# Tokens in a used block sum, row blocks normalised in place, and a fourth buffer of raw weights, in a gated cross-attention and FFN kernel

## The chip, the cores and the metric

The kernel runs on one core of a Trainium2 chip. The metric is the device time of one execution in microseconds (us), median of several runs. PE is the matrix engine (TensorE), DVE the vector engine, ACT the scalar engine, POOL GpSimd and SP the engine that here only issues transfers. [...]

## The reference

There are 8 batches of 256 tokens of width 1024, each with 256 feature rows. A cross-attention with a gated residual is followed by a feed-forward layer with fake-quantised (rounded to 8-bit steps) inputs and weights. Cut to what matters:

```python
# attention, per batch
Q = layernorm(x) @ Wq.T + bq
K = ctx @ Wk.T + bk
attn = softmax(Q @ K.T / sqrt(1024))
x = x + tanh(g_xattn) * (attn @ ctx)
# feed-forward; fake_quant rounds each row to multiples of max|row| / 127
xq = fake_quant(layernorm(x))
h = silu(xq @ fake_quant(w_gate).T) * (xq @ fake_quant(w_up).T)
x = x + tanh(g_ffn) * (fake_quant(h) @ fake_quant(w_down).T)
```

The inner width of the feed-forward layer is 2752, in 22 blocks of up to 128.

## The kernel before

The kernel multiplies the two projection matrices once: M = Wq^T Wk (the tile `mt`), so that scores are x M ctx^T plus bias terms. M is made from seven half-size products of blocks A (of Wq) and B (of Wk) and their sums, in the order P1, a second product, P6, P5, P4, P3, P7 (lines 361 to 481). The sum S1 = A21 + A22 is an input of P5 (line 383) and is not read after it. `usum` and `v_bc` hold bias-weighted column sums; `usum` is read by `bias_columns` in the first two steps of P3.

Up to line 911 every instruction goes out in the order in which the program writes it (`manual_schedule`), on every engine and every queue. This order is by hand, and so is the place of each piece of background work in it.

The background work is the quantisation of the feed-forward weights. `pieces` (lines 180 to 185) lists 92 of them: for every block of 128 rows a gate and an up piece, and, in between, for each of eight blocks of `w_down` three pieces of kind "max" and three of kind "store". `prepare()` (line 247) advances a software pipeline by one step. In step i, piece i-3 is stored (ACT takes the rounding constant off into `rq`, then either SP transposes `rq` into the resident weights, or ACT sends it to `wdq_dram`), piece i is loaded by SP into a `raw` buffer, and piece i-2 is scaled (DVE takes the absolute maximum of each row and the scale from it, POOL multiplies and rounds). For kind "max" only the maximum is taken; for kind "store" only POOL works, with the scale known. Three `raw` buffers are there, so the load of piece i waits until ACT has read piece i-3. The padding of the last `w_down` columns is a memset on POOL.

Before the batch loop, the first batch's tokens `x0` are loaded (line 441) into a tile of the pool `f_right` that has the tag "fn"; the first batch's features (line 600) use the same tag and so the same memory. Then the tokens are normalised and transposed into `xT` (PE transposes into a "tr" bank, of which there are two; ACT or DVE copies it out). The eight query products (`queries_product(j)`, line 499, eight accumulating groups of matmuls from `mt` and `xT`, each evacuated by ACT into H) follow at lines 604 to 617. Between them stand the prepare steps, the statistics of the next batch's tokens (DVE, with a root on ACT), their normalisation, and the transposes of the features into `fT`.

The batch loop (lines 643 to 693) overlaps batch b's softmax and attention with batch b+1's query products. `softmax_stage` (line 619) runs the scores of the two row blocks on PE. Between them PE transposes the next tokens and ACT copies them to `xT`; DVE takes the row maximum (`shift`) and ACT the exponentials (`numerators`). ACT works in order: the first exponential stands between the copies of the first and the second token block. `tokens_bias` (line 426) multiplies tokens by `v_bc` and sums; its product is thrown away, and only the sum is kept. `residual` adds the attention output to the tokens `xr`; the result goes to `x2_dram` from POOL's queue. `steps` (line 575) normalises a row block of `xr` into a tile `y`, takes its scale and scales it; `store_steps` (line 590) has ACT turn it into `xq` (bf16) and sends it out. The second row block's `store_steps` is put off to the next batch (`waiting`). `y` has one buffer, which `scratch` (the thrown-away product) shares.

After the loop the last batch's softmax and attention are mixed with the first blocks of the feed-forward layer (lines 872 to 911). The feed-forward layer then runs to the end: gate and up products, their hidden values, and down products, for eight batches.

Of the kernel before, what the change touches and what calls it, by code (L numbers as in the profile page):

```python
# [9 lines left out]
F32 = mybir.dt.float32  # L10
# [17 lines left out]
def gated_xattn_ffn_kernel(  # L28
# [137 lines left out]
    if True:  # L166
        wraw = keep_scope.enter_context(tc.tile_pool(name="wraw", bufs=3, side=right))
        wkeep = keep_scope.enter_context(tc.tile_pool(name="wkeep", bufs=1, side=right))
# [56 lines left out]
        def prepare_store(i):  # L225
            src, kind, part, r = pieces[i]
            raw = raws.pop(i)
            if kind == "max":
                return
            rq = wraw.tile([P, D], BF16, name="rq", tag="rq", bufs=2)  # L230
            if src is w_down:
                cols = down_cols[part]
                w = cols.stop - cols.start
                nc.scalar.activation(rq[:, :w], raw[:, :w], AF.Identity, bias=nmagic)
                if part == len(down_cols) - 1:

                    nc.gpsimd.memset(rq[:, w : w + NFC * P - FF], 0.0)
                    w += NFC * P - FF
                nc.scalar.dma_start(
                    out=wdq_dram[r][:, cols.start : cols.start + w], in_=rq[:, :w]  # L240
                )
            else:
                n = rows_of(r)
                nc.scalar.activation(rq[:n], raw[:n], AF.Identity, bias=nmagic[:n])  # L244
                nc.sync.dma_start_transpose(out=chunk_of(kind, r), in_=rq[:n])

        def prepare(n=1):
            for _ in range(n):
                i = step[0]
                if 0 <= i - 3 < len(pieces):  # L250
                    prepare_store(i - 3)
                if i < len(pieces):
                    prepare_load(i)
                if 0 <= i - 2 < len(pieces):
                    prepare_scale(i - 2)
                step[0] += 1
# [8 lines left out]

        KH = KC // 2
        wqk_scope = ExitStack()
        wqk = wqk_scope.enter_context(tc.tile_pool(name="wqk", bufs=1))
# [47 lines left out]

        usum = wqk.tile([P, D], F32, name="usum")
        halves = [slice(h * HB, (h + 1) * HB) for h in range(NH)]
# [62 lines left out]
        for k in range(KH):  # L381
# [3 lines left out]
            add(C22[k], p5, C12[k])  # L385
            prepare()
        for k in range(KH):
            p4 = bank("a")
# [37 lines left out]
        def tokens_bias(b, tokens, prod):  # L426
# [8 lines left out]
        cq = {}  # L435
        f_right = keep_scope.enter_context(
            tc.tile_pool(name="f_right", bufs=1, side=right, reuse_waits="tile")
        )

        x0 = f_right.tile([P, NTT, D], F32, name="x0", tag="fn", bufs=1)  # L440
        nc.sync.dma_start(out=x0, in_=x[0].rearrange("(t p) d -> p t d", p=P))
        x0 = [x0[:, t, :] for t in range(NTT)]
        xT = f_right.tile([P, KC, NTT * P], F32, name="xT", tag="xT")
        stats = Rows()
# [130 lines left out]
        def steps(i, xr, stats):  # L575
            y = work.tile([P, D], F32, name="y", tag="y", bufs=1)
            normalise(y, xr, stats, i % NTT)
            scaled(i, y, nc.vector)
            return y

        def normalised_by_scalar(xr, stats, t):
            y = work.tile([P, D], F32, name="y", tag="y", bufs=1)
            nmr = small.tile([P, 1], F32, name="nmr", tag="nmr")
            nc.vector.tensor_scalar(
                nmr, stats.mv[:, t, 0:1], stats.rstd[:, t : t + 1], -1.0, ALU.mult, ALU.mult
            )
            nc.scalar.activation(y, xr, AF.Identity, bias=nmr, scale=stats.rstd[:, t : t + 1])
            return y

# [6 lines left out]
        def scratch():  # L596
            return work.tile([P, D], F32, name="prod", tag="y", bufs=1)


        load_features(0, f_right)  # L600
        xn = load_tokens(1, "xn")
        load_features(1, f_left)
        stats = Rows()
        for j in range(KC):
# [8 lines left out]
            if j in (4, 5):  # L613
                normalise(xn[j - 4], xn[j - 4], stats, j - 4)
            if j in (3, 4):
                features_transposed(0, 2 * j - 6, nc.scalar.copy)
                features_transposed(0, 2 * j - 5, nc.vector.tensor_copy)

# [18 lines left out]
        def queries_between(j):  # L637
            queries_product(j)
            if 0 < j < KC - 1:
                prepare()  # L640

        waiting = None
        for b in range(B - 1):
            nums = softmax_stage(b, xn)
            if waiting:
                store_steps(*waiting)
            prepare()
            queries_between(0)
            xr = load_tokens(b, "xr")
            tokens_bias(b + 1, xn, scratch)  # L650
            pT = numerators_transposed(nums[0][0])
            queries_between(1)
            pas = attend(b, pT)
# [218 lines left out]
    first = {"xq": load_quantised(0), "sx": sx01[:, 0:1, :], "h": []}  # L872
    xr = load_tokens(B - 1, "xr")
    nums = softmax_stage(B - 1, None)
    store_steps(*waiting)
    for r in range(KC):
        nc.sync.dma_start_transpose(
# [148 lines left out]
```

## Time and profile before

| what | value |
|---|---|
| median of 3 runs | 968.78 us (968.43 to 970.61) |
| the profiled execution, whole | 967.01 us |
| its span, first to last instruction | 964.8 us |
| mean granted PE clock | 0.996 of full speed |
| PE idle before 108 us / 108 to 144 / 144 to 476 / 476 to 530 / after 530 | 1.4 / 4.5 / 5.7 / 3.2 / 13.1 us |
| mean share of the 16 DMA engines from 108 to 144 / 144 to 476 us | 0.85 / 0.77 |
| load of a `raw` block, issue to landing | 4.6 us median, 8.3 at most |

The profile is of one execution, whose time is beside its span above; sums over the span are held against that execution. Rows of a timeline give the start and the duration of an instruction in us, its engine, its line, its operation, the tile written and the tiles read, and in brackets how long the engine stood idle before it and what released it. A row of the waits gives the engine and line that waited, what it waited for, the total in us, how many times, and the longest. The projection part ends at about 108 us, the query products ahead of the loop at about 144, the batch loop at about 476.

### The profile page before, as it was taken

The page shows a single profiled execution, that of the slowest core. Times are in us where ns is not written, and L with a number is a line of the kernel's source. Part 1 is how long each engine was busy: PE and PEld are TensorE (multiplying, and loading weights), DVE is VectorE, ACT ScalarE, POOL GpSimd, SP SyncE. Part 2 cuts the span into 40 slices and gives each one's busy share as a digit, 9 for nine tenths or more (in the row PEclk, how much of TensorE's full clock was granted, in tenths as well). Part 3 has the DMA queues.
Part 4 walks back from the last instruction along what each step waited for, and adds up shares of the span by engine and source line. Part 5 has one row for each costly group of instructions (what it writes and reads, how often), then busy time and mean ns, then how long its engine had stood idle before and what let it go on. Part 6 is the DMA issues. An engine that isn't in the chain of part 4 may idle for free.

```text
span 964.8 us, 14230 instructions
## 1 busy us (share of the span) xinstructions
PE 936.9 (97%) x5479; PEld 693.2 (72%) x5496; DVE 645.1 (67%) x1328; ACT 368.4 (38%) x650; POOL 153.5 (16%) x161
## 2 busy tenths in 40 slices
PE   9999989989999999999998899999999999999998
PEld 5444767868787878787877676858768586786854
DVE  5977645768586968777367756666576755767673
ACT  0122325444544535453537753423424143241420
POOL 0031211121221221223000002003030020302005
PEclk9999999999999999999999999999999999999999
DMA  9165976959596977858681611012120121201104
GB/s 347 68 144 181 264 178 190 295 188 314 173 299 203 291 238 249 272 194 256 174 164 34 120 23 65 24 22 89 22 86 3 22 88 23 88 1 45 44 1 153
DMA packets 125699, 135.93 MB, mean 141 GB/s; under 512 B 90241, under 2 KB 91521, under 8 KB 125633
## 3 DMA queue, kind: packets, MB, share of 16 engines
q1 hardware_dynamic: 112352, 104.36, 39.5%
q0 software_dynamic: 4784, 16.52, 4.5%
q10 hardware_dynamic: 8496, 14.16, 4.0%
q8 instruction: 43, 0.70, 0.3%
q14 instruction: 24, 0.19, 0.1%
HBM read 87.04 MB, written 26.74 MB: 118 GB/s over the span
## 4 chain that ended last, share of the span: by engine, by line
PE 78%; DVE 10%; DMA 6%; ACT 3%; issue 2%; SPq 1%; POOL 1%; ACTq 0%; DVEq 0%; POOLq 0%
PE ps_g L746 14%; PE ps_tr L746 14%; PE ps_g L503 11%; PE ps_s L839 6%; PE ps_a L839 6%; PE ps_s L503 6%; PE ps_a L550 6%; PE ps_s L521 4%; PE ps_s L308 3%; PE ps_a L308 3%; PE ps_tr L401 2%; DMA A<-in_L_xattn_Wq_dram 2%; DMA raw<-in_L_ffn_w_up_dram 1%; DMA xr<-x_dram 1%; DVE st L132 1%
## 5 line engine op out<-in xcount | busy, mean ns | idle before, releaser
L503 PE MATMUL ps_g<-xT,mt 128*128 128x256 f32 x640 | 146.4, 382 | 3.4 <-ACT xT L424 3.4
L757 ACT ACTIVATE g<-g,swg 128x256 f32<-128x256 f32 (+1 forms) x176 | 79.7, 499 | 159.3 <-DVE g L755 159.3
L503 PEld LDWEIGHTS ps_g<-xT,mt 128*128 128x128 f32 x640 | 121.0, 192 | 24.3 <-ACT xT L424 5.5
L839 PEld LDWEIGHTS <-hq 128*128 128x128 bf16 x726 | 71.4, 98 | 76.1
L859 POOL TENSOR_TENSOR o<-o,xr 128x512 f32<-128x512 f32 x31 | 39.9, 1288 | 395.3 <-DVE o L856 386.2
L767 DVE SCALAR_TENSOR_TENSOR h<-ps_tr,swu,g 128x256 f32<-128x256 f32 x160 | 70.3, 482 | 43.8 <-ACT g L757 40.6
L746 PE MATMUL ps_tr<-xqb,wuT_lo 128*128 128x256 bf16 x704 | 86.2, 276 | 3.4 <-DVE h L767 3.4
L209 POOL TENSOR_SCALAR raw<-raw,inv 128x1024 f32<-128x1024 f32 (+1 forms) x44 | 56.6, 1286 | 203.9 <-DVE inv L114 139.7
L503 PE MATMUL ps_s<-xT,mt 128*128 128x256 f32 x384 | 86.9, 379 | 0.0
L746 PE MATMUL ps_g<-xqb,wgT_lo 128*128 128x256 bf16 x704 | 84.7, 273 | 0.1
L781 DVE TENSOR_TENSOR acc<-acc,g 128x512 f32<-128x512 f32 (+2 forms) x88 | 56.6, 644 | 41.8 <-ACT g L771 41.0
L746 PE MATMUL ps_tr<-xqb,wuT_hi 128*128 128x256 bf16 x640 | 77.7, 273 | 1.3 <-DVE h L767 1.1
L746 PEld LDWEIGHTS <-wuT_lo 128*128 128x128 bf16 x704 | 69.6, 99 | 12.5 <-issue 3.7
L746 PE MATMUL ps_g<-xqb,wgT_hi 128*128 128x256 bf16 x640 | 77.7, 273 | 0.4 <-DVE g L755 0.4
L503 PEld LDWEIGHTS ps_s<-xT,mt 128*128 128x128 f32 x384 | 71.3, 190 | 8.8
L746 PEld LDWEIGHTS <-wgT_lo 128*128 128x128 bf16 x704 | 69.0, 98 | 9.9 <-issue 0.6
L244 ACT ACTIVATE rq<-raw,nmagic 128x1024 bf16<-128x1024 f32 (+1 forms) x44 | 50.5, 1148 | 65.4 <-POOL raw L209 58.7
L824 DVE TENSOR_TENSOR h<-h,bc 128x512 f32<-128x512 f32 x80 | 51.7, 687 | 28.0 <-ACT bc L819 28.0
L746 PEld LDWEIGHTS <-wuT_hi 128*128 128x128 bf16 x640 | 62.6, 98 | 9.1 <-issue 1.8
L746 PEld LDWEIGHTS <-wgT_hi 128*128 128x128 bf16 x640 | 62.6, 98 | 8.0 <-issue 0.7
L118 DVE TENSOR_REDUCE wam<-raw 128x1 f32<-128x1024 f32 (+1 forms) x44 | 53.1, 1208 | 19.0 <-DMA raw<-in_L_ffn_w_up_dram 18.7
L521 PE MATMUL ps_s<-fT,H 128*128 128x256 f32 x256 | 59.3, 380 | 1.3 <-ACT H L507 1.3
(179 smaller groups left out, 1337.8 us busy)
## 6 DMA issues: line engine op xcount, KB each, us to landing
raw<-in_L_ffn_w_down_dram SPq DMA_DIRECT2D x32, 512.0 KB, 5.3
raw<-in_L_ffn_w_gate_dram SPq DMA_DIRECT2D x21, 512.0 KB, 4.5
raw<-in_L_ffn_w_up_dram SPq DMA_DIRECT2D x21, 512.0 KB, 4.5
fn<-in_ctx_dram SPq DMA_DIRECT2D x8, 1024.0 KB, 8.2
xr<-in_x_dram SPq DMA_DIRECT2D x16, 512.0 KB, 5.5
x_dram<-xr POOLq DMA_DIRECT2D x16, 512.0 KB, 5.7
xr<-x_dram SPq DMA_DIRECT2D x32, 256.0 KB, 3.5
out_dram<-o POOLq DMA_DIRECT2D x31, 256.0 KB, 3.7
```

The source lines that it names most:

```text
L118: nc.vector.tensor_reduce(dst, src, AX.X, ALU.max, apply_absolute_value=True)
L209: nc.gpsimd.tensor_scalar(raw[:n], raw[:n], inv, MAGIC, ALU.mult, ALU.add)
L308: nc.tensor.matmul(pm, lhsT=a[:, c, k * P : (k + 1) * P], rhs=b[:, c, :], start=start, stop=stop)
L503: nc.tensor.matmul(ph, lhsT=mt[:, k, j * P : (j + 1) * P], rhs=xT[:, k, :], start=(k == 0), stop=(k == KC - 1),)
L521: nc.tensor.matmul(ps[:, :L], lhsT=H[:, j, t * P : (t + 1) * P], rhs=fT[:, j, :], start=(j == 0), stop=(j == KC - 1),)
L550: nc.tensor.matmul(pas[h], lhsT=pT[:, l, :], rhs=f_tiles[b][:, l, halves[h]], start=(l == 0), stop=(l == NLT - 1),)
L746: nc.tensor.matmul(pb[:, i, :], lhsT=w[:, k, :], rhs=block["xq"][:, k, :], start=(k == 0), stop=(k == KC - 1),)
L757: nc.scalar.activation(g[:n, i, :], g[:n, i, :], AF.Silu, scale=swg[:n, c : c + 1])
L767: nc.vector.scalar_tensor_tensor(h[:n, i, :], src, swu[:n, c : c + 1], g[:n, i, :], ALU.mult, ALU.mult)
L781: nc.vector.tensor_tensor(acc[:n, i, :], acc[:n, i, :], g[:n, i, :], ALU.max)
L824: nc.vector.tensor_tensor(h, h, ib.to_broadcast((P, 2, TB)), ALU.mult)
L839: nc.tensor.matmul(pds[t, half][:, cols], lhsT=hq[p][:, i, t * P : (t + 1) * P], rhs=wd[:, half * HB + cols.start : half * HB + cols.stop] ...
```

## The change

The first batch's tokens are loaded into the memory of S1, after P5 in program order, in two transfers. The first batch's features are loaded where the tokens were, and the second batch's in step j = 3 of the query products. The features' transposes are spread over j = 2 to 5, all copied by ACT. `f_right` and `xT` are made earlier, and `usum` becomes a view of `xT`.

`raw` gets a fourth buffer, and in a prepare step the load is issued ahead of the store. The padding is written by ACT as ones times zero.

`y` is gone: the normalisation and scaling of `xr` are done in place, and the thrown-away product of `tokens_bias` goes to the `xq` tile, in bf16. `tokens_bias` moves ahead of the put-off `store_steps`. The prepare step that came after `store_steps` moves behind the transpose of the numerators. The one behind query product 1 in the loop is dropped, and one is added behind query product 7. In the last batch the tokens are loaded after `store_steps` and not before the softmax stage.

```diff
--- before.py
+++ after.py
@@ -164,7 +164,7 @@
     order.enter_context(tc.manual_schedule())
     keep_scope = ExitStack()
     if True:
-        wraw = keep_scope.enter_context(tc.tile_pool(name="wraw", bufs=3, side=right))
+        wraw = keep_scope.enter_context(tc.tile_pool(name="wraw", bufs=4, side=right))
         wkeep = keep_scope.enter_context(tc.tile_pool(name="wkeep", bufs=1, side=right))
         mt = wkeep.tile([P, KC, D], F32, name="mt")
         u_col = wkeep.tile([P, KC], F32, name="u_col")
@@ -234,8 +234,9 @@
                 nc.scalar.activation(rq[:, :w], raw[:, :w], AF.Identity, bias=nmagic)
                 if part == len(down_cols) - 1:
 
-                    nc.gpsimd.memset(rq[:, w : w + NFC * P - FF], 0.0)
-                    w += NFC * P - FF
+                    pad = NFC * P - FF
+                    nc.scalar.activation(rq[:, w : w + pad], ones[:, :pad], AF.Identity, scale=0.0)
+                    w += pad
                 nc.scalar.dma_start(
                     out=wdq_dram[r][:, cols.start : cols.start + w], in_=rq[:, :w]
                 )
@@ -247,10 +248,10 @@
         def prepare(n=1):
             for _ in range(n):
                 i = step[0]
+                if i < len(pieces):
+                    prepare_load(i)
                 if 0 <= i - 3 < len(pieces):
                     prepare_store(i - 3)
-                if i < len(pieces):
-                    prepare_load(i)
                 if 0 <= i - 2 < len(pieces):
                     prepare_scale(i - 2)
                 step[0] += 1
@@ -264,6 +265,10 @@
 
 
         KH = KC // 2
+        f_right = keep_scope.enter_context(
+            tc.tile_pool(name="f_right", bufs=1, side=right, reuse_waits="tile")
+        )
+        xT = f_right.tile([P, KC, NTT * P], F32, name="xT", tag="xT")
         wqk_scope = ExitStack()
         wqk = wqk_scope.enter_context(tc.tile_pool(name="wqk", bufs=1))
 
@@ -314,7 +319,7 @@
 
 
 
-        usum = wqk.tile([P, D], F32, name="usum")
+        usum = xT[:, : D // (NTT * P), :].rearrange("p c t -> p (c t)")
         halves = [slice(h * HB, (h + 1) * HB) for h in range(NH)]
 
         def bias_sums(a, b, cs, c, half):
@@ -384,6 +389,13 @@
             combined(T4, T2, B21, ALU.subtract, k)
             add(C22[k], p5, C12[k])
             prepare()
+
+        x0 = [S1[:, 2 * t : 2 * t + 2, :] for t in range(NTT)]
+        for t in range(NTT):
+            nc.sync.dma_start(
+                out=x0[t], in_=x[0, t * P : (t + 1) * P, :].rearrange("p (c d) -> p c d", c=2)
+            )
+        x0 = [v.rearrange("p c d -> p (c d)") for v in x0]
         for k in range(KH):
             p4 = bank("a")
             product_of(p4, A22, k, T4)
@@ -433,14 +445,7 @@
             nc.vector.tensor_scalar(cq[b], cq[b], bqbk, None, ALU.add)
 
         cq = {}
-        f_right = keep_scope.enter_context(
-            tc.tile_pool(name="f_right", bufs=1, side=right, reuse_waits="tile")
-        )
-
-        x0 = f_right.tile([P, NTT, D], F32, name="x0", tag="fn", bufs=1)
-        nc.sync.dma_start(out=x0, in_=x[0].rearrange("(t p) d -> p t d", p=P))
-        x0 = [x0[:, t, :] for t in range(NTT)]
-        xT = f_right.tile([P, KC, NTT * P], F32, name="xT", tag="xT")
+        load_features(0, f_right)
         stats = Rows()
         for k in range(KH):
             p3 = bank("s")
@@ -573,19 +578,17 @@
                 nc.scalar.activation(y, y, AF.Identity, bias=magic, scale=inv)
 
         def steps(i, xr, stats):
-            y = work.tile([P, D], F32, name="y", tag="y", bufs=1)
-            normalise(y, xr, stats, i % NTT)
-            scaled(i, y, nc.vector)
-            return y
+            normalise(xr, xr, stats, i % NTT)
+            scaled(i, xr, nc.vector)
+            return xr
 
         def normalised_by_scalar(xr, stats, t):
-            y = work.tile([P, D], F32, name="y", tag="y", bufs=1)
             nmr = small.tile([P, 1], F32, name="nmr", tag="nmr")
             nc.vector.tensor_scalar(
                 nmr, stats.mv[:, t, 0:1], stats.rstd[:, t : t + 1], -1.0, ALU.mult, ALU.mult
             )
-            nc.scalar.activation(y, xr, AF.Identity, bias=nmr, scale=stats.rstd[:, t : t + 1])
-            return y
+            nc.scalar.activation(xr, xr, AF.Identity, bias=nmr, scale=stats.rstd[:, t : t + 1])
+            return xr
 
         def store_steps(i, y):
             b, t = divmod(i, NTT)
@@ -594,12 +597,10 @@
             nc.scalar.dma_start(out=xq_dram[b][t * P : (t + 1) * P, :], in_=xq)
 
         def scratch():
-            return work.tile([P, D], F32, name="prod", tag="y", bufs=1)
-
-
-        load_features(0, f_right)
+            return work.tile([P, D], BF16, name="prod", tag="xq", bufs=1)
+
+
         xn = load_tokens(1, "xn")
-        load_features(1, f_left)
         stats = Rows()
         for j in range(KC):
             queries_product(j)
@@ -612,9 +613,10 @@
                 stats.inverse()
             if j in (4, 5):
                 normalise(xn[j - 4], xn[j - 4], stats, j - 4)
-            if j in (3, 4):
-                features_transposed(0, 2 * j - 6, nc.scalar.copy)
-                features_transposed(0, 2 * j - 5, nc.vector.tensor_copy)
+            if j == 3:
+                load_features(1, f_left)
+            if j in (2, 3, 4, 5):
+                features_transposed(0, j - 2, nc.scalar.copy)
 
         def softmax_stage(b, xn):
 
@@ -636,19 +638,19 @@
 
         def queries_between(j):
             queries_product(j)
-            if 0 < j < KC - 1:
+            if j > 1:
                 prepare()
 
         waiting = None
         for b in range(B - 1):
             nums = softmax_stage(b, xn)
+            tokens_bias(b + 1, xn, scratch)
             if waiting:
                 store_steps(*waiting)
-            prepare()
             queries_between(0)
             xr = load_tokens(b, "xr")
-            tokens_bias(b + 1, xn, scratch)
             pT = numerators_transposed(nums[0][0])
+            prepare()
             queries_between(1)
             pas = attend(b, pT)
             pT = numerators_transposed(nums[1][0])
@@ -870,9 +872,9 @@
 
     last = (B - 1) * NTT
     first = {"xq": load_quantised(0), "sx": sx01[:, 0:1, :], "h": []}
-    xr = load_tokens(B - 1, "xr")
     nums = softmax_stage(B - 1, None)
     store_steps(*waiting)
+    xr = load_tokens(B - 1, "xr")
     for r in range(KC):
         nc.sync.dma_start_transpose(
             out=wd_early[:, :, r * P : (r + 1) * P], in_=wdq_dram[r][:, : CA * P]
```

## The prediction

> **What bounds the kernel now.** First the busy shares, then who TensorE (PE) waits for. The page and PE's own waits:
>
> ```profile
> PE 936.9 (97%) x5479; PEld 693.2 (72%) x5496; DVE 645.1 (67%) x1328; ACT 368.4 (38%) x650; POOL 153.5 (16%) x161
> ```
> ```profile
> PE ps_tr L401 <- ACT fT L424: 4.5, 2, 3.9
> ...
> PE ps_g L503 <- ACT xT L424: 3.4, 4, 1.8
> ...
> PE ps_tr L401 <- DVE xn L151: 1.2, 1, 1.2
> ```
>
> PE is the bound; no edit changes a matmul, so the change can only win or lose in PE's gaps (27.9 us in all, 13.1 of them after 530 us, where nothing is edited). Two places before 475 us matter.
>
> Place one is the eight query products ahead of the batch loop. PE in order of time, then the stretches with the granted clock:
>
> ```profile
> 122.54 3.62 PE L503 MATMUL ps_s<-xT,mt 128*128 128x256 f32 x16
> 130.03 0.66 PE L401 MATMUL ps_tr<-ident,fn 128*128 128x128 f32 x4 [3.87 <-ACT fT L424]
> 131.36 1.11 PE L401 MATMUL ps_tr<-ident,fn 128*128 128x128 f32 x4 [0.68 <-ACT fT L424]
> 132.27 4.87 PE L503 MATMUL ps_g<-xT,mt 128*128 128x256 f32 x16
> 136.98 3.62 PE L503 MATMUL ps_s<-xT,mt 128*128 128x256 f32 x16
> ```
> ```profile
> 130.00:135.00 5.00, 4.29 (x15) 3.53 (x16) 4.86 (x11) 0.94 (x2) 0.00 (x0) 0.66 0.98 256
> ```
>
> The gap also drops the clock to 0.66, so the next product takes 4.87 instead of 3.62. The stage runs from 107.75 to 143.88 = 36.13 us; undisturbed it is 8 products of 3.455 (start to start) and 4 quarters of transposes of 0.437 = 29.39. **Lost: 6.7 us.** The chain of waits says why, and the VectorE (DVE) timeline agrees:
>
> ```profile
> 116.24 8.30 DMA raw<-in_L_ffn_w_up_dram
> ...
> 124.57 1.23 DVE wam L118
> ```
> ```profile
> 124.57 1.22 DVE L118 TENSOR_REDUCE wam<-raw 128x1 f32<-128x1024 f32 x1 [12.06 <-DMA raw<-in_L_ffn_w_up_dram]
> ```
>
> Read it backwards: PE waits for ACT's copy of fT; ACT stands in order behind the square root of the row statistics; those stand on DVE behind the absolute maximum of a raw weight block, which stood 12.06 us for its load. That load was issued at 116.24, behind a transpose waiting on SP, into DMA engines already over 1.0 busy (115 to 125 us) with 3 MB of tokens and features issued from 107.55 on.
>
> Place two is the softmax stage, once per batch. From the start of the scores to q0 (product 0) it takes 8.66 us undisturbed (stages 0 and 6). Stages 1 to 5 take 12.20, 8.85, 11.12, 9.45, 8.70: **7.0 us lost**, 3.5 of it in stage 1 and 2.5 in stage 3. DVE ahead of stage 1:
>
> ```profile
> 177.71 1.22 DVE L118 TENSOR_REDUCE wam<-raw 128x1 f32<-128x1024 f32 x1 [3.13 <-DMA raw<-in_L_ffn_w_up_dram]
> ...
> 183.88 1.22 DVE L118 TENSOR_REDUCE dam<-raw 128x1 f32<-128x1024 f32 x1 [1.50 <-DMA raw<-in_L_ffn_w_down_dram]
> ...
> 199.55 0.41 DVE L529 TENSOR_REDUCE nm<-ps_s 128x1 f32<-128x256 f32 x1
> ```
>
> From 183.88 to 199.55 DVE has no gap; the scores were done at 192.8, but their maximum comes 6.7 us later, exp after it, and on ACT the copies of xT after exp, for which q0 waits. 4.63 us of that lateness are the two load waits.
>
> **Front stage, part by part.** x0 moves to S1. S1's last reader is P5, over at 60.7; SP reaches the load after its weight transpose of about 62.4, so 1 MB lands by about 72 (6.4 us when it was issued at 75.20). Its first reader is the statistics at 87.31: 15 us of cover. usum in xT: last read at 82.2, xT first written at 102.8: nothing. Features 0 take the place of x0's load at 75, land by about 84, and are first read after product 2 (118): 34 us of cover. Features 1 go to SP at about 120 and are first read at 166.8. So 2 of the 3 MB leave the knot at 107.5. In a step the load now stands ahead of the transpose, and with four buffers it waits for the ACT copy of the piece four back, made a step earlier. The load of 116.24 can so go at about 109 (its piece four back was copied at 104.01 to 105.2) and lands by 115 to 117 (4.6 us, the median for raw blocks, up to 8.3, the maximum). DVE is then free for the token statistics at about 117, the root's input is there by 120, and ACT asks for it after product 3 (122). Four copies of fT go to ACT, one per product (0.57 each); the two it takes over from DVE are hidden under 3.45 of product. I take all of it: **-6.7**. If the load stays late by 3 us, PE still has two "tr" banks and the products up to 7 between: 0 is lost until the root is some 10 us late.
>
> **The loop.** Ten prepare steps per batch before and after, but the second now follows the numerators' transpose and the others slide, the last to behind product 7. So between the second residual and the next softmax maximum DVE has one weight reduction with scales more (1.21+0.15+0.16 = 1.53) when that piece is a gate or up block or a down maximum, by the list of pieces in stages 1, 2, 3 and (1.22, unhurt, as stage 6 has slack) 6; in 4 and 5 it is a piece without DVE work. Against it, each load has nearly one more step (3.5 us) between landing and use.
> - Stage 1: DVE's own work from 171.5, added up from its rows with one reduction more and no load wait, ends its maximum at 197.3 instead of 200.4. The normalise that held the transposes 1.20 is done by 190.6. **-3.0**.
> - Stage 2: +1.53, minus two load waits of 0.63: maximum 0.3 later. **+0.3**.
> - Stage 3: +1.53, minus 1.5 of load and contention waits: DVE even. Product 7's copy (H) no longer stands behind the weight copy that cost PE 1.29, but that copy (1.15) now stands between H and xT: about 1 us of it comes back through the two "tr" banks. **-0.5**.
> - Stages 4 to 6: DVE has the same sum or slack: 0.
>
> **In place on xr.** The normalise must now wait for the store of x2 from the same rows. Stores leave POOL's queue at 169.65/180.60, 217.65/227.11 and so on to 445.05/455.34; normalises come 9.6 to 21 us after (tightest: 455.34 to 464.99); landing took 2.7 to 8.2. Hidden; uncovered, a late store would hold DVE and all behind it, us for us. At the end 490.73 landed in 7.1 and ACT normalises at 508.40: hidden.
>
> **tokens_bias earlier, bf16 scratch.** No row has this output. Nearest is the same instruction, 1.23; ACT shows 1.24 for f32 output and 1.15 for bf16, so 1.14 to 1.23; I take 1.23, off the path. It now stands ahead of ACT's xq copy, behind which H of product 0 and the copy of pT wait: in stage 3 that copy ends about 301.5 and the attend matmuls want it at about 301.9. Hidden by 0.4 there, 1 to 3 elsewhere; a DVE instruction doubled by POOL (2.02 was seen) would cost up to 1 each.
>
> **xr's loads behind the store.** Here a rule speaks against the change. The row: SP stood for ACT weight copies 21 times, 101.4 us in all, and the wait of DVE for xr was 15.3 in 4. The rule (the Trainium skill, "DMA: Bandwidth & Descriptors", Anatomy of one DMA): a DMA engine never waits on a semaphore, the issuing sequencer does, so xr[1]'s load, waiting for xq, holds every weight load behind it. By the rule alone about 3 us of delay per stage for the step behind. By the rows SP was held at that place anyway (load at 205.10, xr at 205.48, freed by ACT at 205.1), and xq now ends at about 205. I take 0; xr[0], ahead of the hold, even comes earlier. In the last batch the hold puts the eight wd_early transposes 7 us later (472.21 to about 479); they are read from 571 on: 0.
>
> **Padding on ACT.** Eight activations of 128x64: between 0.20 (128x2) and 0.47 (128x256), taken 0.28, ACT is 38% busy: 0. POOL loses a memset that stood 30.1 us in 4, in nobody's way.
>
> **Sum:** -6.7 -3.0 +0.3 -0.5 = -9.9. On the profiled execution 967.01 (span 964.8 and 2.2 around) that is 957.1; it lies 1.8 under the median of the runs, so 968.78 - 9.9 = 958.9, say **959.0**.
>
> **Rivals.** (a) Only the front gain: load-ahead is eaten by the slid steps and stage 1 keeps its waits. 968.8 - 6.7 = 962. For it: loads wait for an ACT copy in both orders. Against: front and loop loads have different cover. (b) The gap moves: DVE waits elsewhere for the same bytes and gives back nearly all, 967 to 968. For it: DMA is 0.7 to 1.0 busy all along; against: PE needs no byte before it is late. (c) **Slower:** the step behind product 7 puts 1.53 on DVE ahead of the maximum and 1.15 on ACT ahead of xT, in series, in all six stages: 6 x 2.7 = 16.1, stage 1 gains nothing, -6.7 stays: 978. It decides from 1.1 us per stage net (6.7/6). For it: stages 1 and 3 are held by exactly this chain. Against: stages 5 and 6 have DVE or ACT slack.
>
> **Numbers.** Forecast 0.58 (own range 956 to 961.5), (a) 0.20, (b) 0.08, (c) 0.14. About 0.2% (2 us) is what can be told from no change. Faster 0.78, same 0.08, slower 0.14. Low 955 is all 13.7 us of both places; high 968 leaves out (c) and little else.
>
> **What would show it.** Right: no fT wait over 1 us, clock 1.00 between 125 and 150, eight products in about 29.5 us, stage 1 under 10 us, no DVE wait for x2's store. Wrong: a DVE wait for raw or tokens of over 5 us between 110 and 125; q0 waiting for xT by over 2 us in stages 2 to 5; PE waiting for pT.

## The result, and the profile after

| | before | after |
|---|---|---|
| median of 6 runs each, us | 967.89 (967.22 to 970.61) | 962.81 (959.20 to 964.21) |
| ratio, 95% interval | | 0.9935 [0.9913, 0.9957] |
| profiled execution, us (span) | 967.01 (964.8) | 959.20 (957.1) |

The change makes the kernel about 5 us faster, half of the 9.9 that were forecast. The same kernel measured again in 17 runs beside the experiments below gave 963.59 and a ratio of 0.9969 [0.9959, 0.9979], so the gain was nearer 3 us in that set; the two intervals don't meet, and why is open. The profiled run is the fastest of its six, its span 7.7 us below before's; by its own timeline the gap to before is 5.34 us at the last batch's scores (463.63 against 468.97). The 2.4 us beyond that come where nothing is edited, and are not the change's (last section).

The page of after, then PE's own waits (total, times, longest):

```profile
PE 934.1 (98%) x5496; PEld 691.3 (72%) x5496; DVE 641.6 (67%) x1326; ACT 370.0 (39%) x660; POOL 149.6 (16%) x153
```
```profile
PE ps_g L508 <- ACT xT L436: 4.5, 5, 1.8
...
PE ps_tr L413 <- ACT xT L436: 2.8, 2, 2.1
```

The waits for fT (4.5 us) and for xn (1.2) are gone. The wait of product 0 for xT has grown from 3.4 to 4.5, and a new one stands beside it: the transposes wait for the copies of xT that should free their banks. Two readings follow.

**Place one, the front.** PE in order of time, the window 130 to 135 us (its eighth number is the granted clock), and the DVE row of the raw load:

```profile
121.83 0.60 PE L413 MATMUL ps_tr<-ident,fn 128*128 128x128 f32 x4
122.26 3.62 PE L508 MATMUL ps_s<-xT,mt 128*128 128x256 f32 x16
...
129.61 0.60 PE L413 MATMUL ps_tr<-ident,fn 128*128 128x128 f32 x4
130.05 3.62 PE L508 MATMUL ps_s<-xT,mt 128*128 128x256 f32 x16
```
```profile
130.00:135.00 5.00, 5.00 (x25) 4.42 (x24) 0.00 (x0) 1.31 (x3) 2.95 (x3) 1.00 0.85 343
```
```profile
114.02 1.22 DVE L118 TENSOR_REDUCE wam<-raw 128x1 f32<-128x1024 f32 x1 [1.79 <-DMA raw<-in_L_ffn_w_up_dram]
```

No bracket of waiting stands behind a PE row, each product takes 3.62, the clock is 1.00 where it was 0.66, and the load's wait is 1.79 instead of 12.06. From first product (107.47) to scores (136.96) it is 29.49 us instead of 36.13.

**Place two, the softmax stages.** Scores' start to product 0, against 8.66 undisturbed:

| stage | 1 | 2 | 3 | 4 | 5 | sum over 8.66 |
|---|---|---|---|---|---|---|
| before | 12.20 | 8.85 | 11.12 | 9.45 | 8.70 | 7.0 |
| after | 10.65 | 9.95 | 11.46 | 10.65 | 9.29 | 8.7 |

Stage 1 gained half of what was forecast, the other four lost. Product 0 waits for the last copies of xT; on ACT these stand behind the first exponential, which waits for VectorE's first shift: the maximum of each row and two operations on one column. In nine of the ten cells above product 0 starts 1.12 to 1.13 us after the shift's end (in stage 3 of after 1.20), so the shift shows what each stage lost. From VectorE's rows:

| stage | 1 | 2 | 3 | 4 | 5 |
|---|---|---|---|---|---|
| maximum begins, us after the scores, before | 10.23 | 6.87 | 9.13 | 7.47 | 6.72 |
| the same, after | 8.16 | 7.46 | 9.40 | 8.16 | 6.80 |
| last operation of the shift takes, before | 0.16 | 0.16 | 0.16 | 0.16 | 0.16 |
| the same, after | 0.67 | 0.67 | 0.16 | 0.68 | 0.68 |
| weight reductions between second residual and maximum, before / after | 5 / 6 | 5 / 6 | 5 / 6 | 5 / 5 | 3 / 3 |
| waits for ACT's square root there, before / after | 0.27 / 1.40 | 0.27 / 0.93 | 0.27 / 1.47 | 0.67 / 1.34 | 3.13 / 2.74 |

Stage 4 has the same number of reductions in both kernels and still loses 1.20. DVE in before, then DVE and POOL in after:

```profile
321.16 0.17 DVE L143 RECIPROCAL rr<-rt 128x2 f32<-128x2 f32 x1 [0.67 <-ACT rt L138]
...
339.34 0.42 DVE L529 TENSOR_REDUCE nm<-ps_s 128x1 f32<-128x256 f32 x1
...
340.04 0.16 DVE L531 SCALAR_TENSOR_TENSOR nm<-cq,nm 128x1 f32<-128x1 f32 x1
```
```profile
313.13 0.17 DVE L143 RECIPROCAL rr<-rt 128x2 f32<-128x2 f32 x1 [1.34 <-ACT rt L138]
...
331.32 1.21 DVE L118 TENSOR_REDUCE wam<-raw 128x1 f32<-128x1024 f32 x1
...
332.90 0.41 DVE L534 TENSOR_REDUCE nm<-ps_s 128x1 f32<-128x256 f32 x1
...
333.59 0.68 DVE L536 SCALAR_TENSOR_TENSOR nm<-cq,nm 128x1 f32<-128x1 f32 x1
```
```profile
333.14 1.12 POOL L209 TENSOR_SCALAR raw<-raw,inv 128x1024 f32<-128x1024 f32 x1 [3.18 <-DVE inv L114]
```

The maximum begins 0.69 later, as VectorE stood 0.67 longer for the square root of the row statistics. The shift's last operation takes 0.52 longer and ends at 334.27, with GpSimd's scaling (334.26). The scales for that scaling come from the prepare step that now stands behind product 7: a gate block's maximum and scales, 331.32 to 332.90, directly ahead of the softmax maximum. ACT and PE in after:

```profile
329.99 1.15 ACT L245 ACTIVATE rq<-raw,nmagic 128x1024 bf16<-128x1024 f32 x1 [3.75 <-POOL raw L209]
331.05 1.05 ACT L436 COPY xT<-ps_tr 128x512 f32<-128x512 f32 x2
```
```profile
331.67 1.14 PE L413 MATMUL ps_tr<-ident,xn 128*128 128x128 f32 x8 [0.71 <-ACT xT L436]
...
335.39 3.72 PE L508 MATMUL ps_g<-xT,mt 128*128 128x256 f32 x16 [0.85 <-ACT xT L436]
```

The scores that the maximum at 332.90 reads have been there since about 328.4. The same step's rounding on ACT (329.99) stands ahead of the first xT copies; ACT had waited 3.75 us for GpSimd there. PE has two waits: 0.71 before the transposes, behind that rounding, and 0.85 before product 0, behind the shift. The experiments on the halves of the step tell which of the two counts.

### The profile page after: what moved, and what is told of

Read it like the earlier page. It is cut to its first block, busy times and chain, and to the rows that moved or that the text cites. A ratio compares the mean times of both kernels' runs of the same rounds, so it can differ in the third digit from the quotient of the medians.

```text
span 957.1 us, 14239 instructions
## 1 busy us (share of the span) xinstructions
PE 934.1 (98%) x5496; PEld 691.3 (72%) x5496; DVE 641.6 (67%) x1326; ACT 370.0 (39%) x660; POOL 149.6 (16%) x153
## 4 chain that ended last, share of the span: by engine, by line
PE 80%; DVE 11%; ACT 5%; DMA 2%; issue 1%; POOL 0%; ACTq 0%; DVEq 0%
PE ps_g L748 14%; PE ps_tr L748 14%; PE ps_g L508 10%; PE ps_a L841 7%; PE ps_s L841 7%; PE ps_s L508 5%; PE ps_a L555 5%; PE ps_s L313 4%; PE ps_a L313 4%; PE ps_s L526 2%; PE ps_g L313 2%; PE ps_tr L413 2%; DMA wdq_dram<-rq 2%; DVE wam L118 2%; DVE st L132 1%
## 5 line engine op out<-in xcount | busy, mean ns | idle before, releaser
L209 POOL TENSOR_SCALAR raw<-raw,inv 128x1024 f32<-128x1024 f32 (+1 forms) x44 | 54.6, 1241 | 255.1 <-DVE inv L114 144.4
L566 DVE SCALAR_TENSOR_TENSOR xr<-ps_a,r,xr 128x512 f32<-128x512 f32 x32 | 23.9, 751 | 62.5 <-PE ps_a L555 62.5
L773 ACT ACTIVATE g<-h 128x512 f32<-128x512 f32 x72 | 45.2, 628 | 37.8 <-DVE h L769 37.8
```

Source lines behind the costliest of these rows:

```text
L209: nc.gpsimd.tensor_scalar(raw[:n], raw[:n], inv, MAGIC, ALU.mult, ALU.add)
L773: nc.scalar.activation((acc if p == 0 else g)[:n, i, :], h[:n, i, :], AF.Abs)
```

## The experiments

Three sets of runs, each on one chip beside its own runs of before (966.42 for e0 to e4, 966.82 for e5, e6, f1 and f2, 966.84 us median for f3, f4 and e7), to which the ratios refer. "Excess" is the sum of stages 1 to 5 over 8.66 as in the table above; "loop" runs from the first batch's scores to the last batch's; "front" is the eight products. These three lengths come from one profile each.

| run | median us | ratio [95%] | front | excess | loop |
|---|---|---|---|---|---|
| before | | | 36.13 | 7.0 | 325.1 |
| e0_again | 963.59 | 0.9969 [0.9959, 0.9979] | 29.49 | 9.2 | 327.2 |
| e4_step7_to_0 | 956.85 | 0.9898 [0.9883, 0.9913] | 29.48 | 1.7 | 321.1 |
| e2_steps_into_slack | 964.68 | 0.9989 [0.9977, 1.0001] | 29.49 | 14.8 | 332.6 |
| e3_store_ahead_3_buffers | 966.66 | 0.9995 [0.9981, 1.0010] | 29.49 | 11.7 | 332.5 |
| e5_store_half_late | 962.94 | 0.9960 [0.9945, 0.9976] | 29.49 | 9.9 | 329.3 |
| e6_scale_half_late | 957.35 | 0.9892 [0.9869, 0.9915] | 29.49 | 6.3 | 324.0 |
| f1_features_late_again | 963.15 | 0.9957 [0.9940, 0.9974] | 29.49 | 9.9 | 327.8 |
| f2_moves_alone | 959.54 | 0.9920 [0.9901, 0.9938] | 29.48 | 7.7 | 325.6 |
| f3_tokens_early_alone | 967.27 | 1.0008 [0.9997, 1.0019] | 36.66 | 7.8 | 325.7 |
| f4_load_ahead_alone | 960.80 | 0.9941 [0.9922, 0.9959] | 29.49 | 9.7 | 327.6 |
| e7_step7_3_buffers | 961.76 | 0.9939 [0.9918, 0.9960] | 29.49 | 8.4 | 327.4 |

**The changed kernel again**, no edit, as the yardstick for the others.

> The changed kernel once more, unedited, to set the others beside it. All theories: 0.993 to 0.996 of before (962 to 964 us); scores to first query product 8.7 us over the undisturbed sum in stages 1 to 5; in the tail, 16 matmuls of the first feed-forward product taking 1.9 us where the clock is whole and 3.4 us where it dips.

The ratio came out 0.9969, weaker than expected by a thousandth; the excess is 9.2. In its tail the 16 matmuls take 3.18.

**Is it the step behind product 7?** One step moves:

```diff
-            if j > 1:
+            if 1 < j < KC - 1:
                 prepare()
...
                 store_steps(*waiting)
+            prepare()
             queries_between(0)
```

> The one prepare step behind query product 7 goes ahead of product 0 instead, six times; nothing else moves. Theory A (the step behind product 7 costs the loop its gain: its 1.4 us of maximum and scales stand ahead of the shift on DVE, its GpSimd part runs beside the shift's small operations, its ScalarE part stands ahead of the xT copies): the excess of stages 1 to 5 falls from 8.7 us to 3 to 5, query product 0 waits for xT no longer, and the time falls by 4 to 5 us to about 958. Rival B (the early value bias and the normalising now done in place fill the vector engine ahead of the shift, or the sync queue's 11 us hold does it): the step is not the cause, the excess stays within 1 us of 8.7 and the time within 1 us of the changed kernel.

Theory A, and by more than it asked: 6.7 us under the changed kernel. The early value bias, the rows done in place and the hold on SP all stayed, so rival B is out. PE's waits, and stage 4's rows, VectorE first, then PE:

```profile
PE ps_g L508 <- ACT xT L436: 1.4, 4, 0.6
```
```profile
327.74 0.75 DVE L576 TENSOR_SCALAR xr<-xr,inv 128x1024 f32<-128x1024 f32 x1
328.41 0.42 DVE L534 TENSOR_REDUCE nm<-ps_s 128x1 f32<-128x256 f32 x1
...
329.11 0.16 DVE L536 SCALAR_TENSOR_TENSOR nm<-cq,nm 128x1 f32<-128x1 f32 x1
```
```profile
330.40 3.72 PE L508 MATMUL ps_g<-xT,mt 128*128 128x256 f32 x16 [0.57 <-ACT xT L436]
```

The softmax maximum follows the row block's scaling at once, and the shift's last operation takes 0.16 in all five stages. The transposes' wait for xT no longer appears among PE's waits, product 0 waits 1.4 us in all instead of 4.5. Stages 1 to 5 lose 7.5 us of excess against e0 (9.2 to 1.7): 1.85, 1.44, 2.38, 1.26 and 0.58. In the program one step moves, but the steps take their pieces in order, so every step from the first residual on has the piece again that it had before: stages 1 to 3 are back at five reductions, and the waits for the square root at 0.6 to 0.7 in stages 1 to 4. The move isn't entirely free: PE now waits three times for pT, 0.7 us in all, and the loop gets shorter by 6.1, not 7.5. This version beats both kernels.

**Which engine's part of the step?** Half of it goes behind the first shift, into the step that stands inside the softmax stage:

```diff
-                if 0 <= i - 3 < len(pieces):
+                if 0 <= i - 3 < len(pieces) and off != "store":
                     prepare_store(i - 3)
...
+                if b and 0 <= step[0] - 4 < len(pieces):
+                    prepare_store(step[0] - 4)
                 prepare()
...
-                prepare()
+                prepare(off="store" if j == KC - 1 and b < B - 2 else None)
```

and the same with prepare_scale, i - 2 and step[0] - 3 for the other half.

> Of the step behind product 7, the store half alone (ScalarE's rounding of an earlier block and the transpose it feeds) is put off to the step inside the softmax stage, behind the second pair of xT copies; its load and its maximum stay. Theory A1 (the vector engine's part is the price: the maximum ahead of the shift delays the exponentials and the xT copies behind them): little changes, 0 to 1.5 us against 963.6, excess of stages 1 to 5 at 7.5 to 9. Theory A2 (the ScalarE part is the price: the rounding waits 3.2 to 3.8 us for GpSimd and holds the xT copies): the transposes' waits of 2.1 and 0.7 us in stages 3 and 4 go, the excess falls to 4 to 6 and the time by 3 to 5 us to 959 to 961.

> Of the step behind product 7, the scale half alone (the vector engine's maximum and scales, or GpSimd's scaling) is put off to the step inside the softmax stage, between the two shifts; load and store stay. Theory A1: the first shift comes 1.4 us sooner in each stage, the excess of stages 1 to 5 falls to 3 to 6 and the time by 3 to 5 us to 959 to 961, the second shift now being the late one by up to 0.5 us. Theory A2: the waits of the xT copies for the rounding stay, the excess falls by less than 1.5 and the time by less than 1.5 us.

PE's waits with the store half late, then with the scale half late:

```profile
PE ps_g L508 <- ACT xT L436: 9.0, 6, 2.8
```
```profile
PE ps_tr L413 <- ACT xT L436: 2.8, 2, 2.1
...
PE ps_g L508 <- ACT xT L436: 0.9, 2, 0.6
```

Theory A1. Taking ScalarE's rounding out of the way removes the transposes' wait (no row of it is left), and product 0's wait takes its place, 9.0 us instead of 4.5 to 5.0. No gain is shown: 962.94 beside 963.59, from different sets, and the intervals of the ratios overlap. The last xT copies were late anyway, behind an exponential that stood for the shift; in stages 4 and 5 the shift ends 9.52 and 8.16 us after the scores, in e0 9.52 and 8.17. Taking VectorE's half away keeps the transposes' 2.8 and yet wins 6.2 us. The wait that the profile puts on the ScalarE copy was VectorE's. The edit moves the reduction and the GpSimd scaling together; the rows tell them apart. In stage 4 the maximum begins 1.58 sooner than in e0 (6.58 after the scores, not 8.16), and the shift's last operation takes 0.16 instead of 0.67.

**Can VectorE's idle time take more steps?**

```diff
-            if j > 1:
+            if 0 < j < KC - 2:
                 prepare()
...
             residual(b * NTT, pas, xr[0], nums[0][1])
-            prepare()
+            prepare(2)
```

> No prepare step behind products 6 and 7; one behind product 1 and a second one after the first residual, where the vector engine idles up to 10 us a stage. Theory A: the excess of stages 1 to 5 falls to 0 to 3 us and the time by 5 to 8 us to 955 to 958, since nothing of a step is left between the maximum and the shift. Rival B: no change beyond 1 us. Rival C (the steps only move the wait, from xT to pT or to the attention's evictions): the excess falls but the stretch from product 7 to the next scores grows by as much, and the time stays within 1 us.

None of the three: product 0's wait fell to 1.2 us, but the excess rose to 14.8. PE in stage 1, then the DVE row behind it:

```profile
189.76 1.16 PE L413 MATMUL ps_tr<-ident,xn 128*128 128x128 f32 x8 [2.90 <-DVE xn L151]
190.72 3.53 PE L526 MATMUL ps_s<-fT,H 128*128 128x256 f32 x8
```
```profile
177.02 1.22 DVE L118 TENSOR_REDUCE dam<-raw 128x1 f32<-128x1024 f32 x1 [2.38 <-DMA raw<-in_L_ffn_w_down_dram]
```

The idle time lies ahead of the residuals, which wait for the attention's matmuls; a step put behind the first residual comes after it. The two steps taken from behind products 6 and 7 now stood ahead of the normalising of xn, with loads issued closer together (the 2.38), and the transposes became the late ones. Product 0's slot in e4 is ahead of the residuals: their idle time for PE falls from 62.5 (after) to 41.0 (another 15.0 in e4 is for the load of xr):

```profile
DVE xr L566 <- PE ps_a L555: 41.0, 24, 5.6
```

**What are the fourth buffer and the load ahead worth?** In the changed kernel, and in e4's version:

```diff
-        wraw = keep_scope.enter_context(tc.tile_pool(name="wraw", bufs=4, side=right))
+        wraw = keep_scope.enter_context(tc.tile_pool(name="wraw", bufs=3, side=right))
...
-                if i < len(pieces):
-                    prepare_load(i)
                 if 0 <= i - 3 < len(pieces):
                     prepare_store(i - 3)
+                if i < len(pieces):
+                    prepare_load(i)
```

> The raw pool back at three buffers with the store ahead of the load in each step; all other parts of the change stay. Theory D (the moves of tokens and features alone empty the queue in the front stage): query products still take 29.5 us in the front, no vector wait over 2 us for a raw load there, and the time is within 1 us of the changed kernel. Theory E (the fourth buffer is what lets the raw load be early enough): a wait of 3 to 10 us for a raw load comes back in the front, the products take 32 to 36 us and the time rises by 3 to 7 us.

> The version with product 7's step ahead of product 0, but three buffers and the store ahead of the load. If the fourth buffer pays in the loop: load waits on the vector engine in stage 1 return (3 us or more in all), its scores to product 0 go from 9.1 to 11 to 13, and the time rises by 2 to 4 us to 959 to 961. If it doesn't: within 1 us of 956.9.

Both times they pay: 3.1 us and 4.9 us. Of e3's theories, D is right on the front's length (29.49), though not on its waits: a raw wait of 5.68 is there, where it allowed 2, and costs nothing. It is wrong on the total; in the profile nearly all of the loop's loss is in and behind stage 1: 13.15 instead of 10.98, and behind its 3.31 us wait 16 matmuls take 6.47 instead of 3.62. In e7, VectorE's waits for raw loads return in three rows that e4 showed at 2.0 and 1.3 us in all (the first two) or not at all:

```profile
DVE wam L118 <- DMA raw<-in_L_ffn_w_up_dram: 12.3, 6, 5.6
DVE dam L118 <- DMA raw<-in_L_ffn_w_down_dram: 10.0, 8, 1.7
...
DVE wam L118 <- DMA raw<-in_L_ffn_w_gate_dram: 1.4, 3, 0.7
```

**Which move closed the front's gap?** Four ways: the features put back (f1), the moves alone on the kernel before (f2), the tokens' move alone (f3), and everything but the moves (f4).

```diff
f1, on after
-        load_features(0, f_right)
         stats = Rows()
...
+        load_features(0, f_right)
         xn = load_tokens(1, "xn")
+        load_features(1, f_left)
...
-            if j == 3:
-                load_features(1, f_left)
```
```diff
f3, on before (f2: the features' lines as in after as well)
-        x0 = f_right.tile([P, NTT, D], F32, name="x0", tag="fn", bufs=1)
-        nc.sync.dma_start(out=x0, in_=x[0].rearrange("(t p) d -> p t d", p=P))
-        x0 = [x0[:, t, :] for t in range(NTT)]
...
+        x0 = [S1[:, 2 * t : 2 * t + 2, :] for t in range(NTT)]
+        for t in range(NTT):
+            nc.sync.dma_start(
+                out=x0[t], in_=x[0, t * P : (t + 1) * P, :].rearrange("p (c d) -> p c d", c=2)
+            )
+        x0 = [v.rearrange("p c d -> p (c d)") for v in x0]
```

f4 is f1 with these tokens' lines taken back too.

> The changed kernel with both feature loads back beside the load of the second batch's tokens, where they were; first tokens in the used sum, buffers and steps as changed. Theory M (three large loads at one point are what the raw load queued behind): the front's products take 32 to 36 us, a vector wait of 5 us or more for a raw load comes back, the time rises by 3 to 7 us to about 968. Rival N (the tokens' move and the load ahead are enough): products 29.5 us, time within 1 us of 963.6.

> The kernel before with only the moves of the loads: first tokens into the used sum, features 0 early, features 1 behind product 3; three buffers, store ahead of load, the steps in their old places. Theory M: the front's products take 29.5 us, the softmax stages keep their excess of 7.0 (within 1), and the time is 6 to 7 us below before, about 960. Rival: a wait for a raw load stays in the front or turns up in stage 1, and the gain is under 3 us.

> The kernel before with one edit: the first batch's tokens are loaded into the used sum at its end of life; features, buffers, steps as before. If taking 1 MB of 3 out of the knot is enough: the front's products take 29.5 us and the time is about 6 us below before. If the features' move was needed too: the wait of some 12 us for the raw load shrinks to no less than 6, the products take 32 to 36 us and the gain is under 4 us.

> The changed kernel with tokens and both features loaded where they were before; fourth buffer, load ahead of store, in-place rows and the new step places stay. If the load ahead alone empties the front's wait (issued at about 109 in place of 116): products 29.5 us and the time within 1 us of the changed kernel. If the 3 MB at one point are what counts: a vector wait of 8 us or more stays, products 33 to 36 us, and the time is 4 to 7 us above the changed kernel, near or over before.

The DVE row of the raw load with the tokens' move alone, and PE behind it:

```profile
125.93 1.22 DVE L118 TENSOR_REDUCE wam<-raw 128x1 f32<-128x1024 f32 x1 [11.69 <-DMA raw<-in_L_ffn_w_up_dram]
```
```profile
131.39 1.11 PE L407 MATMUL ps_tr<-ident,fn 128*128 128x128 f32 x4 [3.47 <-ACT fT L430]
133.18 1.12 PE L407 MATMUL ps_tr<-ident,fn 128*128 128x128 f32 x4 [0.68 <-ACT fT L430]
134.08 5.33 PE L506 MATMUL ps_g<-xT,mt 128*128 128x256 f32 x16
```

and the DVE row with the load ahead alone:

```profile
119.51 1.22 DVE L118 TENSOR_REDUCE wam<-raw 128x1 f32<-128x1024 f32 x1 [7.20 <-DMA raw<-in_L_ffn_w_up_dram]
```

The tokens' move alone does nothing: the gap of the kernel before stands there in full. The features' move with the tokens' (f2, wait 4.90) closes it, and so does the load ahead without any move of a load (f4, wait 7.20) or with the tokens' alone (f1, 6.83). The two remedies are alternatives, not two halves. A wait that ends 11.9 us after the first product (119.51 less 107.57) costs nothing; one that ends 16.4 us after it (125.93 less 109.50) costs 7.2.

One difference was not tried alone: f1 and f4 keep the transposes spread over j = 2 to 5, f2 and f3 have them in j = 3 and 4. An estimate from the rows of before says that the spread isn't what saves f4. There PE goes on 5.46 us after the wait's end (124.57 to 130.03), and had been ready 18.4 us after the first product; f4's wait, over at 11.9, would let it go on at 17.4.

M of f1 and the second reading of f4 are wrong, and so is the first reading of f3; M of f2 came, with a gain of 7.3 us where it said 6 to 7. f4's time is 2.8 us under e0's, where its first reading allowed 1; its front and loop are e0's within 0.4, and what the rest is stays open. The features' move without the tokens' was not tried: there they share a buffer. f2 ends 7.3 us under before: the moves alone gain at least as much as the whole change (0.9920 beside 0.9935 and 0.9969), and their loop is before's within 0.5, since the steps keep their places.

## Why the prediction was right and wrong

The sign was right, and the time lay in the range; the number was missed by 3.8 us, with 962.81 outside the likeliest case's own range and on rival (a)'s 962. The front alone carries the gain. The loop's term had the wrong sign, -3.2 against +1.7, and the time stayed in the range only because the range, 955 to 968, was wide enough for rival (a).

The step that failed is in that term. It added up VectorE's own work and its waits for loads, and the count of reductions is right in all six stages. It put at nothing VectorE's waits for ACT's square root, and it took the shift's last operation as undisturbed beside GpSimd. Over stages 1 to 5 the first measured 3.27 more than before (7.88 instead of 4.61), the second 2.06; the term was missed by 4.9. When the step moves (e4) the first shrinks to 5.76 and the second is gone; it is gone too when only the step's VectorE half moves (e6). Why ACT's square root came later in each stage no run took apart; in stage 4 a rounding, the padding (0.24) and a table load stand ahead of it from 310.19 to 312.88.

- **The front, -6.7:** right. 36.13 fell to 29.49, -6.64, with the clock at 1.00 and no fT wait. The load went out at 107.68 (said: about 109). The working, though, credited the moves and the load ahead together, and either alone is enough. Its cover of "some 10 us" for the root was not tried: in f4 the root on ACT comes at 125.49, 2.05 later than in after, and is free.
- **Stage 1, -3.0:** measured -1.55. The load waits went as said, and the sixth reduction was in the sum. The waits for ACT's square root were not: 1.40 instead of 0.27. Nor was the shift's last operation, 0.67 instead of 0.16 beside the scaling that the slid step's scales release. Together that is 1.64, and 1.45 was missing. DVE and POOL in stage 1 of after:

```profile
182.30 0.17 DVE L143 RECIPROCAL rr<-rt 128x2 f32<-128x2 f32 x1 [0.73 <-ACT rt L138]
...
190.47 0.41 DVE L534 TENSOR_REDUCE nm<-ps_s 128x1 f32<-128x256 f32 x1
...
191.16 0.67 DVE L536 SCALAR_TENSOR_TENSOR nm<-cq,nm 128x1 f32<-128x1 f32 x1
```
```profile
190.71 4.07 POOL L221 TENSOR_SCALAR raw<-raw,inv 128x1024 f32<-128x1024 f32 x3 [14.80 <-DVE inv L114]
```

  With the step moved away (e4) stage 1 is 9.13, 3.07 below before. That this meets the -3.0 is chance: the forecast counted six reductions, e4 has five.
- **Stages 2 and 3, +0.3 and -0.5:** measured +1.10 and +0.34, with 0.66 and 1.20 more of waiting for the square root; the shift's last operation adds 0.51 in stage 2 and nothing in stage 3, where the slid piece releases no scaling. Without the step (e4) the stages take 8.65 and 9.15, below before both. The "about 1 us" through the two transpose banks came as 2.07 of wait.
- **Stages 4 to 6, 0:** "a piece without DVE work" was right for 4 and 5, where the number of reductions is the same before and after. "The same sum" did not make the same time: 0.67 more of waiting for the square root in stage 4 and 0.52 at the shift in each cost 1.20 and 0.59. Stage 6, with one reduction more, cost nothing, as said.
- Together the loop's term was -3.2 by the working and +1.7 in the stages' table (loop 325.09 to 326.67). With the front that makes -6.64, another -0.28 from the first product's earlier start, and +1.58, which is the -5.34 of the timeline. The place had been written down, in rival (c): ahead of the maximum, decisive "from 1.1 us per stage net". By e4 against e0 the slid steps cost 0.58 to 2.38 a stage, 6.7 us of time. They were set against a load ahead that is worth nearly as much in the loop (e4 against e7: 4.9 us), so the two nearly cancelled. That is rival (a): "load-ahead is eaten by the slid steps". Its other half, "stage 1 keeps its waits", did not come.
- **In place, bf16 scratch, padding, at 0:** nothing against them. DVE never waits for a store of x2; the scratch took 1.21 to 1.23 (said 1.23), twice 1.75 beside GpSimd, with no wait of PE behind it; the padding took 0.24 to 0.25 (said 0.28).
- **xr's loads behind the store, at 0:** nothing speaks against it. The rule of the Trainium skill that was weighed ("DMA: Bandwidth & Descriptors", Anatomy of one DMA: the issuing sequencer waits, not the DMA engine) is what the trace shows, on SP in stage 1:

```profile
186.37 11.03 SPq L521 DMA_DIRECT2D xr<-in_x_dram  x2
```

  SP stood 11 us there, and DVE's wait for xr, 15.3 us before, is gone from the list all the same: the rule holds, and no price of it shows. No run took the hold away. In e4 the wait is back at 15.0 us in 3, and none of PE's waits is put down to it.

With the one step moved the kernel stands 9.6 us under before (956.85 against 966.42). That this is the forecast's -9.9 within 0.3 is partly chance, since the moved step leaves VectorE less to do ahead of the maximum than the forecast had counted; but the change had that much in it, and the place of its steps took the loop's share.

## What to carry to other kernels

When background work slides by a slot, write out for each stage what it puts ahead of the operation with the tightest deadline, on which engine, from the actual list of its pieces; an engine at 67% has slack at one place (here ahead of the residuals) and none at another (ahead of the softmax maximum), and one step moved from the second to the first was worth 6.7 us. Counting that engine's own work is not enough: with equal counts stage 4 still lost 1.20, to a wait for another engine and to a neighbour's work beside a small operation. A wait named for one engine's copy may be another's lateness: taking the copy's rival away (e5) only moved the wait, taking away the reduction, with the scaling that it releases (e6), won the time. When a change carries two remedies for one gap, try each alone before keeping both.

## What was not expected of the hardware

Equal waits of PE do not cost the same. The transposes' wait of 2.07 us in stage 3 is in after and in e6, and the scores behind it take 1.89 in the first and 3.54 in the second. After, then e6:

```profile
285.11 1.14 PE L413 MATMUL ps_tr<-ident,xn 128*128 128x128 f32 x8 [2.07 <-ACT xT L436]
286.09 1.89 PE L526 MATMUL ps_s<-fT,H 128*128 128x256 f32 x8
```
```profile
282.86 1.22 PE L413 MATMUL ps_tr<-ident,xn 128*128 128x128 f32 x8 [2.07 <-ACT xT L436]
283.87 3.54 PE L526 MATMUL ps_s<-fT,H 128*128 128x256 f32 x8
```

The granted clock of e6 in the window 280 to 290 us is 0.83; in after it is 1.00 from 282 to 292. Of six profiles with this wait (2.06 or 2.07 us), e0 and e3 are like after, and f1 (3.53) and f4 (3.09) more like e6. The 2.84 us wait in the unedited tail does likewise: the 16 matmuls behind it take 3.40 in the profile of before, 1.91 in that of after, and 3.18 in after's second profile. The 1.5 us between the first two are most of the 2.4 that the profiled runs differ by beyond the change.

The Trainium skill ("TensorE: Matmul & The Clock Gate", Part 1) has the clock set by the activity in a free-running window and halved after an idle window of about 3.4 us. Waits of 2.07 and 2.84 us are shorter, and the clock fell after some of them all the same; here the measurement decides. That it hangs on where in the window a wait falls would fit, but no run here shows the window. A short wait on PE can thus cost about 1.5 us more in one run than in another, which limits what a profile of one run can tell; e6's excess of 6.3 has 1.65 of it.
